# Group-norm sums between the steps of a convolution stack: operands in float32r pieces, and the mean's sum one step later

## The chip, the cores and the metric

The kernel runs on one core of one Trainium2 chip. The metric is the time of one execution on the device, in microseconds; a result is the median of several runs. Engines have names in the profile: PE is TensorE (PEld its weight loads), DVE is VectorE, ACT is ScalarE, POOL is GpSimd, SP is SyncE, which issues most transfers.

## The reference: what is computed

The input `x` has four batches of 32 x 32 points with 16 channels. Three layers of the same kind come first, each `x = x + conv(gn(x))`. `gn` is a group norm: for each batch and each pair of channels, mean and variance are taken over all 1024 points and both channels.

```
g = v.reshape(B_, H_, W_, G, C_ // G)
m = jnp.mean(g, axis=(1, 2, 4), keepdims=True)
s = jnp.var(g, axis=(1, 2, 4), keepdims=True)
return ((g - m) / jnp.sqrt(s + eps)).reshape(v.shape)
```

The convolution has its own 3 x 3 filter `G` for each of the 1024 points that it looks from; what each filter makes of the whole image is subtracted from the input, cut off at zero, weighted with `Wp` and summed; a term with `M` is added. The fourth layer is a long two-dimensional filter whose taps come from a quotient of Fourier transforms. It too begins with a group norm.

## The kernel before, in words

**Layout.** The 128 partitions of an activation tile are eight rows of points times sixteen channels; the free axis has four batches of 128 points each. The batches are worked on in two pairs: pair 0 is batches 0 and 1, pair 1 is batches 2 and 3.

**A layer.** `conv_layer` (L433) goes through 128 blocks, eight to a chunk of weights. What is called a step here is one block for one batch: six matmuls (L470): two row halves of 64 partitions for each of three weight tiles. `ga` and `gb` are float32, `gn` is float32r. Each float32 matmul leaves two records in the profile, each float32r matmul one, so a step has ten records. They accumulate in a pair of PSUM banks. VectorE then reduces the pair against the weights `wt` (L478, output `junk`, the sum in `acc`). The PSUM pool holds four such pairs (`pair_psum`, L70), for the group norm's sums too.

**The order is written by hand.** Nothing is planned: instructions stand on each engine in the order in which the Python code issues them. After each step, `step()` (L426) moves every generator in the list `todo` to its next `yield`. That is how side work gets between the steps.

**The ends of a pair.** The jobs of a layer are sorted so that pair 0 ends eight blocks (sixteen steps) before pair 1 does: in the first two and the last two jobs, only one pair is worked on. When a pair is done, VectorE adds the result to the residual (L493), and `finish` is put on `todo` and moved once at once. In layers 0 and 1 `finish` is `make_image` (L268): a group norm, then `store_image` (L276), which writes the normalised pair to DRAM (L288 on SP, L289 and L290 on ACT), then `load_image` (L292), which loads it again in 24 shifted copies through SP, ACT and POOL (L301). The next layer's matmuls on that pair need these copies. In layer 2 `finish` is `norm3` (L730), which normalises into VectorE's own tiles for the last filter. Other side work of the page, such as `beside` (L440), isn't touched.

**The group norm.** `group_norm` (L108) has four parts, with `yield` between them: statistics of the pair (`bn_stats`, L116); sums of the means over partitions by TensorE, then the mean and the deviations `d` on VectorE (L121 to L128); sums of `d`; the variance and its inverse root (L133 to L144). `group_sums` (L98) makes the sums: one float32 matmul of the operand with the constant table `avg` for each row half, `lhsT=avg[rows], rhs=s[rows]` (L105). For a pair the operand has four columns. `norm3` uses another way for pair 1, `column_sums` (L733). The first norm of all, in `first_images` (L167), is over four batches at once, before the first step; `rest` (L239) inside it is side work of the first steps.

Between the mean's sums and the variance's, `make_image` has two steps (two `yield`s, L129 and L130). `norm3` has one for pair 0, since it takes the first of the two itself.

Of the kernel before, what the change touches and what calls it, by code (L numbers as in the profile page):

```python
# [29 lines left out]
F32 = mybir.dt.float32  # L30
F32R = mybir.dt.float32r
AF = mybir.ActivationFunctionType
ALU = mybir.AluOpType
AX = mybir.AxisListType
# [3 lines left out]
P = 128  # L38
B, C, S = 4, 16, 32
# [15 lines left out]
def conv_stack_kernel(ctx, tc, x, raw, M, W, G, den, num, h0, cst, dft, one, idp, idq, out):  # L55
    nc = tc.nc

    const = ctx.enter_context(tc.tile_pool(name="const", bufs=1))
    xp = ctx.enter_context(tc.tile_pool(name="xp", bufs=2))
    work = ctx.enter_context(tc.tile_pool(name="work", bufs=1))  # L60
    small = ctx.enter_context(tc.tile_pool(name="small", bufs=2))
# [8 lines left out]
    def pair_psum():  # L70
        return ps.tile([P, 2, 512], F32, tag="pt", name="pt")
# [5 lines left out]
    xs = xp.tile([P, B, NBLK], F32, tag="x", name="x")  # L77
    nc.sync.dma_start(out=xs, in_=x)
    cs = const.tile([P, 2 * P + C + 2], F32, name="cs")
    nc.scalar.dma_start(out=cs, in_=cst)  # L80
    ident, avg, mid = cs[:, :P], cs[:, P : 2 * P], cs[:, 2 * P : 2 * P + C]
    is_lo, sign = cs[:, 2 * P + C : 2 * P + C + 1], cs[:, 2 * P + C + 1 :]


# [20 lines left out]
            nc.tensor.matmul(pt[:, h, :n], lhsT=avg[rows], rhs=s[rows], start=True, stop=True)  # L105
        return pt[:, :, :n].rearrange("p h (b e) -> p b h e", e=2), AX.XY

    def group_norm(xt, center=None, sums=group_sums):  # L108


        nb = xt.shape[1]
        vec = lambda name: small.tile([P, B], F32, tag=name, name=name)[:, :nb]

        st = small.tile([P, B, 2, 3], F32, tag="st", name="st")[:, :nb]
        for b in range(nb):
            nc.vector.bn_stats(st[:, b].rearrange("p e k -> p (e k)"), xt[:, b])  # L116
        half, m, m2 = NBLK // 2, st[:, :, :, 1], st[:, :, :, 2]
        yield
        pm, axes = sums(m)
        neg = vec("neg")  # L120
        nc.vector.tensor_reduce(neg, pm, axes, ALU.add)  # L121
        nc.vector.tensor_scalar(neg, neg, -float(half), None, ALU.mult)
        if center:
            center(neg)
        d = small.tile([P, B, 2], F32, tag="d", name="d")[:, :nb]
        nc.vector.tensor_tensor(d, m, neg.unsqueeze(2).to_broadcast([P, nb, 2]), ALU.add)
        nc.vector.tensor_tensor(d, d, d, ALU.mult)
        nc.vector.scalar_tensor_tensor(d, d, float(half), m2, ALU.mult, ALU.add)  # L128
        yield  # L129
        yield  # L130
        pv, axes = sums(d)
        v = vec("v")
        nc.vector.tensor_reduce(v, pv, axes, ALU.add)  # L133
        nc.vector.tensor_scalar(v, v, 1e-5, None, ALU.add)

        r = vec("r")
        nc.scalar.activation(r, v, AF.Sqrt)
        ri = vec("ri")
        nc.vector.reciprocal(ri, r)
        nc.vector.tensor_tensor(ri, ri, v, ALU.mult)  # L140
        nc.vector.tensor_tensor(r, r, ri, ALU.add)
        nc.vector.tensor_scalar(r, r, 0.5, None, ALU.mult)
        rstd = vec("rstd")
        nc.vector.reciprocal(rstd, r)  # L144
        return neg, rstd
# [21 lines left out]
    def first_images():  # L167

        of = lambda t, b: t[:, :, b % 2].rearrange("p l cc x -> p l (cc x)")
        rlo = st.tile([P, B], F32, name="rlo")  # L170

        def center(which, *batches):
            for b in batches:
                v = of(ims[b // 2][which], b)
                nc.scalar.activation(v, v, AF.Identity, bias=neg[:, b : b + 1])  # L175

        def scale(b):
            v = of(ims[b // 2][1], b)
            nc.scalar.activation(v, v, AF.Copy, scale=rstd[:, b : b + 1])  # L179

        def clear(which, a, b=slice(0, 2)):

            top, bottom = (0, 0, slice(0, S)), (3, 3, slice(0, S))
            left, right = ((slice(0, 4), slice(0, 4), slice(x, x + 1)) for x in (0, S - 1))
            parts = {
                0: [(g, g + 16, left) for g in range(0, P, 32)] + [(0, 32, top)],
                1: [(g, g + 32, right) for g in (0, 64)]
                + [(g + 32, g + 48, left) for g in (0, 64)]
                + [(0, 16, top), (96, P, bottom)],
                2: [(0, P, right), (64, P, bottom)],  # L190
            }[which]
            for lo, hi, (l, cc, x) in parts:
                nc.gpsimd.memset(ims[a][which].bitcast(F32)[lo:hi, l, b, cc, x], 0.0)  # L193

        def first_tap(b):
            v = of(ims[b // 2][0], b)
            nc.vector.tensor_scalar(v, v, rstd[:, b : b + 1], None, ALU.mult)

        def last_tap(b):

            v, v8, m = of(nine[b // 2], b), of(ims[b // 2][2], b), neg[:, b : b + 1]
            nc.vector.tensor_scalar(v8, v, m, rstd[:, b : b + 1], ALU.add, ALU.mult)
            yield
            nc.vector.tensor_scalar(v, v, m, rlo[:, b : b + 1], ALU.add, ALU.mult)
            yield
            nc.vector.scalar_tensor_tensor(v8, v8.bitcast(F32), sign, v, ALU.mult, ALU.add)
            clear(2, b // 2, slice(b % 2, b % 2 + 1))

        first, second = (prepare_g(0, 0, part) for part in halves)
        neg = None  # L210

        def early(mean):
            nonlocal neg
            neg = mean
            center(0, 0, 1)
            clear(0, 0)
            next(first)

        norm = group_norm(xs, early)
        while True:  # L220
            try:
                next(norm)
            except StopIteration as end:
                neg, rstd = end.value
                break
        for b in range(2):
            center(1, b)
            clear(1, 0, slice(b, b + 1))
        scale(0)
        first_tap(0)  # L230
        nc.vector.tensor_scalar(rlo, rstd, is_lo, None, ALU.mult)
        list(last_tap(0))
        list(first)
        scale(1)
        first_tap(1)
        list(last_tap(1))
        next(second)

        def rest():  # L239

            yield
            list(second)
            yield
            for which in range(2):
                center(which, 2, 3)
                clear(which, 1)
            yield
            for _ in range(4):
                yield
            for b in (2, 3):  # L250
                scale(b)
                first_tap(b)
                yield
                yield from last_tap(b)
                yield
            for a in range(2):
                normalise(a, xs[:, 2 * a : 2 * a + 2], *(t[:, 2 * a : 2 * a + 2] for t in (neg, rstd)))
                yield

        todo.append(rest())  # L260

    def normalise(a, xt, neg, rstd):
        yc[a] = work.tile([P, 2, NBLK], F32, tag=f"yc{a}", name=f"yc{a}")
        for b in range(2):
            at = slice(b, b + 1)
            nc.vector.tensor_scalar(yc[a][:, b], xt[:, b], neg[:, at], rstd[:, at], ALU.add, ALU.mult)

    def make_image(a, xt):  # L268

        xt = xt[:, 2 * a : 2 * a + 2]  # L270
        neg, rstd = yield from group_norm(xt)
        store_image(a, xt, neg, rstd)
        yield
        load_image(a)
# [114 lines left out]
    def prepare_g(layer, ch, part=slice(0, GC)):  # L389


        at = chunk(layer, ch)
        if at[0] == 3 or (part.start == 0 and at in gt):
            return
        if part.start == 0:
            gt[at] = *gr[at][:2], gs.tile([P, GC, P], F32R, tag="gn", name="gn")
        ga, gb, gn = (t[:, part] for t in gt[at])
        g9 = gr[at][2][:, part]

        gv = ga.rearrange("r n (p f) -> r (n p) f", f=C)  # L400
        nc.gpsimd.tensor_tensor(  # L401
            gv, gv, mid.unsqueeze(1).to_broadcast([P, gv.shape[1], C]), ALU.subtract
        )
        yield
        nc.scalar.copy(gn, g9)  # L405
        for r in (32, 96):
            lo = gn[r : r + 32]
            nc.vector.tensor_tensor(lo, g9[r : r + 32], lo.bitcast(F32), ALU.subtract)  # L408
# [237 lines left out]
    with tc.tile_pool(name="st", bufs=1) as st:  # L646
# [20 lines left out]
        xs = conv_layer(0, xs, make_image, impulse_response())  # L667
    xs = conv_layer(1, xs, make_image)
# [37 lines left out]
    early, then = ([of_pair(a, k, q) for k, q in ((1, 0), (1, 2), (0, 0))] for a in range(2))  # L706
# [23 lines left out]
    def norm3(a, xt):  # L730
# [15 lines left out]
        if a == 0:  # L746
# [1 line left out]
            yp = yp[:, : 16 * (31 + S - FIRST)]  # L748
            late["yp"] = yp.rearrange("p (a cc q b) -> p a cc q b", a=2, cc=4, b=2)
            nc.gpsimd.memset(late["yp"], 0.0)  # L750
        steps = group_norm(xt[:, 2 * a : 2 * a + 2], sums=column_sums if a else group_sums)
        if a:
            xr = work.tile([P, 4, S, B], F32, tag="ft", name="xr")
            nc.scalar.copy(xr, xt.rearrange("p b (cc q) -> p cc q b", q=S))
            late["sides"] = pair_psum()
            bank_of.update({("pair", n): late["sides"][:, n] for n in range(2)})
            run(early[0])
        next(steps)
        yield
        next(steps)  # L760
        if a:
            run(early[1])
# [54 lines left out]
    xs = conv_layer(2, xs, norm3, toeplitz(), late_toeplitz())  # L817
# [5 lines left out]
    pt = pair_psum()  # L823
# [130 lines left out]
```

## Time and profile before

| what | value |
|---|---|
| median of 3 runs | 3122.62 us (3121.87 to 3123.34) |
| the profiled execution's own time | 3123.33 us |
| its span, first to last instruction | 3121.6 us |
| granted TensorE clock | 1.000 |
| group-norm sums at L105, matmul records | 48 (24 on `st`, 24 on `d`) |
| TensorE idle before L105 for the statistics L116 | 7.7 us in 6 places, of them 5.4 us at the start |
| mean of one L478 reduction on VectorE | 1224 ns |

A line of a group of instructions has the source line, the engine, the operation, output and inputs with their shapes, and the count; then the busy time in us and the mean duration in ns; then the engine's idle time just before, and what ended most of it. A line of the chain of waits has the start in us, the duration in us and what ran. A line of the timeline has start, duration, engine, line and operation; a bracket gives the idle time before it and what ended it.

### The profile page before, as it was taken

What the parts mean: (1) busy time and instruction counts of PE and PEld (TensorE: products, weight loads), DVE (VectorE), ACT (ScalarE), POOL (GpSimd) and SP (SyncE); (2) the same over time, 40 slices, a digit from 0 to 9 for tenths busy, and PEclk for the clock granted to TensorE, in tenths of its full rate; (3) what the DMA queues carried; (4) which work ended last, traced back from release to release, by engine and by line L of the source; (5) the groups of instructions that cost most, each with busy time, mean ns of one, the idle gap of its engine ahead of it and who ended that gap; (6) DMA issues with size and microseconds to landing.
All of it is one profiled execution on the core that took longest, in us unless ns stands there. A gap on an engine that the chain in (4) does not pass through costs nothing.

```text
span 3121.6 us, 39186 instructions
## 1 busy us (share of the span) xinstructions
PE 3105.2 (99%) x16264; PEld 1668.7 (53%) x16264; DVE 2066.5 (66%) x3341; ACT 82.4 (3%) x107; POOL 236.8 (8%) x271
## 2 busy tenths in 40 slices
PE   8999999999999999999999999999999999999999
PEld 4445567777777554444444444455444444444444
DVE  7666766666667666666666666766666666666664
ACT  1000000000000000000000000000000000000000
POOL 1012321000000100100000000010010000000000
PEclk9999999999999999999999999999999999999999
DMA  8453355333332654433333333275543444444422
GB/s 216 133 124 87 81 118 123 90 88 88 100 92 66 144 133 131 95 88 88 101 92 88 87 101 91 69 144 128 140 105 97 96 109 107 96 97 106 109 44 42
DMA packets 68406, 322.77 MB, mean 103 GB/s; under 512 B 10514, under 2 KB 17556, under 8 KB 42756
## 3 DMA queue, kind: packets, MB, share of 16 engines
q1 hardware_dynamic: 57280, 301.61, 38.9%
q10 hardware_dynamic: 6612, 10.94, 2.0%
q0 software_dynamic: 4336, 7.72, 1.4%
q8 instruction: 127, 2.08, 0.3%
q14 instruction: 51, 0.42, 0.1%
HBM read 313.82 MB, written 6.41 MB: 103 GB/s over the span
## 4 chain that ended last, share of the span: by engine, by line
PE 99%; DVE 0%; DMA 0%; POOL 0%; issue 0%; ACT 0%; SPq 0%; POOLq 0%; DVEq 0%; ACTq 0%
PE pt L470 96%; PE pt L721 1%; PE pt L335 1%; DVE junk L478 0%; DMA im<-in_raw_dram 0%; PE pt L523 0%; PE pt L566 0%; PE pt L605 0%; PE pt L105 0%; POOL im L193 0%; DVE x L493 0%; DVE st L116 0%; PE pt L323 0%; ACT im L175 0%; ACT im L179 0%
## 5 line engine op out<-in xcount | busy, mean ns | idle before, releaser
L478 DVE SCALAR_TENSOR_TENSOR junk<-pt,w 128x1024 f32<-128x1024 f32 x1536 | 1880.7, 1224 | 993.5 <-PE pt L470 979.5
L470 PE MATMUL pt<-im,ga 64*128 64x512 f32 x6144 | 1676.0, 591 | 3.1 <-POOL im L193 3.1
L470 PE MATMUL pt<-im,gb 64*128 64x512 f32 x6144 | 1668.1, 588 | 0.1
L470 PE MATMUL pt<-im,gn 64*128 64x512 f32 x3072 | 1342.6, 806 | 0.0
L470 PEld LDWEIGHTS pt<-im,gb 64*128 64x128 f32 x6144 | 674.9, 185 | 669.5 <-issue 586.9
L470 PEld LDWEIGHTS pt<-im,ga 64*128 64x128 f32 x6144 | 671.6, 187 | 389.7 <-DVE junk L478 219.5
L470 PEld LDWEIGHTS pt<-im,gn 64*128 64x128 f32 x3072 | 350.6, 186 | 332.7 <-issue 291.5
L401 POOL TENSOR_TENSOR ga<-ga,cs 128x1024 f32<-128x1024 f32 (+2 forms) x49 | 113.5, 2317 | 2088.6 <-DMA ga<-in_G_dram 2088.3
L478 DVE DVE_READ_ACCUMULATOR junk<-pt,w 128x1 f32 x1536 | 127.8, 83 | 0.0
L408 DVE TENSOR_TENSOR gn<-g,gn 32x1024 fp32r<-32x1024 f32 (+2 forms) x98 | 118.4, 1208 | 4.7 <-ACT gn L405 2.5
L405 ACT CAST gn<-g 128x1024 fp32r<-128x1024 f32 (+2 forms) x49 | 50.4, 1029 | 2257.9 <-DMA g<-in_G_dram 1755.4
L359 POOL DMA_DIRECT2D fd<-ft x48 | 25.2, 533 | 223.3 <-DVE ft L352 222.1
L721 PE MATMUL pt<-t,y 128*32 128x512 f32 (+3 forms) x352 | 23.9, 432 | 0.0
L335 PE MATMUL pt<-mt,yt 128*64 128x512 f32 x96 | 21.9, 598 | 0.0
L721 PEld LDWEIGHTS pt<-t,y 128*32 128x32 f32 x352 | 11.0, 110 | 12.7 <-issue 10.8
L842 DVE TENSOR_TENSOR xo<-xo,both 128x512 f32<-128x512 f32 x2 | 1.4, 692 | 23.5 <-DMA both<-sd 23.5
L301 POOL DMA_DIRECT2D im<-img x32 | 16.1, 513 | 8.9 <-DMA img<-y 8.9
L721 PE MATMUL pt<-t,yp 128*32 128x512 f32 (+3 forms) x192 | 13.6, 434 | 0.2 <-DVE yp L771 0.2
L335 PEld LDWEIGHTS pt<-mt,yt 128*64 128x64 f32 x96 | 6.4, 136 | 13.7 <-issue 9.7
L544 POOL TENSOR_TENSOR H<-H,d 128x256 f32<-128x256 f32 (+1 forms) x10 | 8.2, 824 | 68.2 <-DVE d L549 67.8
L284 POOL COPY e<-y 32x612 f32<-32x612 f32 x4 | 2.8, 693 | 126.5 <-DVE y L283 126.5
L544 POOL TENSOR_TENSOR t<-s 128x256 f32<-128x256 f32 (+1 forms) x15 | 11.3, 753 | 0.0
(92 smaller groups left out, 209.2 us busy)
## 6 DMA issues: line engine op xcount, KB each, us to landing
w<-in_W_dram SPq DMA_DIRECT2D x192, 1024.0 KB, 7.5
ga<-in_G_dram SPq DMA_DIRECT2D x47, 512.0 KB, 3.5
gb<-in_G_dram SPq DMA_DIRECT2D x47, 512.0 KB, 4.3
g<-in_G_dram SPq DMA_DIRECT2D x47, 512.0 KB, 7.2
mt<-in_M_dram SPq DMA_DIRECT2D x24, 512.0 KB, 10.0
t<-hd ACTq DMA_DIRECT2D x28, 160.0 KB, 7.4
t<-hd SPq DMA_DIRECT2D x28, 160.0 KB, 8.4
im<-img SPq DMA_DIRECT2D x32, 67.5 KB, 5.4
```

Source lines behind the costliest of these rows:

```text
L284: nc.gpsimd.tensor_copy(ye[a][96:, :, :, 1:, :], ys[a][96:, :, :, :3, :])
L301: (nc.sync, nc.scalar, nc.gpsimd)[n % 3].dma_start(out=ims[a][k][at : at + C] .bitcast(F32) .rearrange("c l b cc x -> c l (b cc x)")[:, :, ...
L335: nc.tensor.matmul(pf[64 * h : 64 * h + 64], lhsT=yt[:, 4 * part + k].rearrange("k b c -> k (b c)"), rhs=mts[k][:, h, :], start=(k == 0), ...
L359: nc.gpsimd.dma_start(out=fv[h, cc, b], in_=ft[at : at + C, cc])
L401: nc.gpsimd.tensor_tensor(gv, gv, mid.unsqueeze(1).to_broadcast([P, gv.shape[1], C]), ALU.subtract)
L405: nc.scalar.copy(gn, g9)
L408: nc.vector.tensor_tensor(lo, g9[r : r + 32], lo.bitcast(F32), ALU.subtract)
L470: nc.tensor.matmul(pt[:, half, :], lhsT=w[rows, blk % GC, :], rhs=im[rows, :, b % 2, :, :S], start=n == 0, stop=n == 2,)
L478: nc.vector.scalar_tensor_tensor(junk, pt.rearrange("p h m -> p (h m)"), 0.0, wt, ALU.min, ALU.mult, accum_out=acc[b // 2][:, b % 2, blk : ...
L544: mul = lambda o, u, w: nc.gpsimd.tensor_tensor(o, u, w, ALU.mult)
L721: nc.tensor.matmul(rows.rearrange("n (j r) -> n j r", j=C)[:, :, 8 * cc :], lhsT=y(cc).rearrange("p q b -> p (q b)"), rhs=ts[k][q][:, :, : ...
L842: nc.vector.tensor_tensor(xo, xo, both[:, bass.ts(i, S * C)], ALU.add)
```

## The change

Two new functions stand beside `group_sums`. `in_pieces` splits a float32 operand into two float32r pieces on VectorE: `hi` is the operand rounded to float32r, and `lo` is what is left of it. The four columns of a pair become eight. `piece_sums` multiplies these eight columns with `avg_r`, a float32r copy of the table `avg`; VectorE's reductions after it (L121 and L133) then add over four instead of two values for each batch. Both hi and lo go through one float32r matmul for each row half.

`group_norm` gets the preparation of the operand as an argument of its own, `operand`, and calls it right after the operand is there. It has one more `yield` between the statistics and the mean's sums. Pieces are what it does unless told otherwise. The first norm of all keeps `group_sums` on the unsplit operand, and so does `column_sums` for pair 1 of `norm3`. The table's copy is made on VectorE at the end of `rest`.

`norm3` runs the first two parts with a step after each for pair 0; for pair 1 it runs them one right after the other, as the one part before.

```diff
+    avg_r = const.tile([P, P], F32R, name="avg_r")
...
-    def group_norm(xt, center=None, sums=group_sums):
+    def in_pieces(s):
+
+        pieces = small.tile([P, B, 2, 2], F32R, tag="pieces", name="pieces")[:, : s.shape[1]]
+        hi, lo = pieces[:, :, 0], pieces[:, :, 1]
+        nc.vector.tensor_copy(hi, s)
+        nc.vector.tensor_tensor(lo, s, hi.bitcast(F32), ALU.subtract)
+        return pieces
+
+    def piece_sums(pieces):
+
+
+        pt = pair_psum()
+        n = 4 * pieces.shape[1]
+        for h in range(2):
+            rows = slice(64 * h, 64 * h + 64)
+            nc.tensor.matmul(
+                pt[:, h, :n],
+                lhsT=avg_r[rows],
+                rhs=pieces[rows].rearrange("p b k e -> p (b k e)"),
+                start=True,
+                stop=True,
+            )
+        return pt[:, :, :n].rearrange("p h (b e) -> p b h e", e=4), AX.XY
+
+    def as_it_is(s):
+        return s
+
+    def group_norm(xt, center=None, operand=in_pieces, sums=piece_sums):
...
         half, m, m2 = NBLK // 2, st[:, :, :, 1], st[:, :, :, 2]
+        to_add = operand(m)
         yield
-        pm, axes = sums(m)
+        yield
+        pm, axes = sums(to_add)
...
         nc.vector.scalar_tensor_tensor(d, d, float(half), m2, ALU.mult, ALU.add)
+        to_add = operand(d)
         yield
         yield
-        pv, axes = sums(d)
+        pv, axes = sums(to_add)
...
-        norm = group_norm(xs, early)
+        norm = group_norm(xs, early, as_it_is, group_sums)
...
+            nc.vector.tensor_copy(avg_r, avg)
...
-        steps = group_norm(xt[:, 2 * a : 2 * a + 2], sums=column_sums if a else group_sums)
+        ways = dict(operand=as_it_is, sums=column_sums) if a else {}
+        steps = group_norm(xt[:, 2 * a : 2 * a + 2], **ways)
...
-        next(steps)
-        yield
+        for _ in range(2):
+            next(steps)
+            if not a:
+                yield
         next(steps)
```

## The prediction

> **What bounds the kernel.** I read the page first: busy times, the shares of the chain that ended last, the costliest groups.
>
> ```profile
> PE 3105.2 (99%) x16264; PEld 1668.7 (53%) x16264; DVE 2066.5 (66%) x3341; ACT 82.4 (3%) x107; POOL 236.8 (8%) x271
> ...
> PE 99%; DVE 0%; DMA 0%; POOL 0%; issue 0%; ACT 0%; SPq 0%; POOLq 0%; DVEq 0%; ACTq 0%
> ...
> L478 DVE SCALAR_TENSOR_TENSOR junk<-pt,w 128x1024 f32<-128x1024 f32 x1536 | 1880.7, 1224 | 993.5 <-PE pt L470 979.5
> ```
>
> TensorE is 99% of the chain; VectorE mostly waits for it. So only what TensorE executes, or waits for, counts. Next, the chain around one end of a batch pair (layer 0 into 1), where the sums of the change stand:
>
> ```profile
> 1009.10 1.24 DVE junk L478 x2
> ...
> 1010.36 0.44 DVE x L493
> ...
> 1010.83 0.50 DVE st L116 x2
> 1011.32 0.14 issue
> 1011.46 0.39 PE pt L105 x4
> 1011.85 4.00 PE pt L470 x18
> 1015.85 0.15 PE pt L105 x2
> ```
>
> Here the chain leaves TensorE: it goes through the last reduction of the pair, the residual addition L493 and the statistics L116 before the mean sums (L105) may start. The variance sums at 1015.85 have no VectorE piece ahead of them. The timeline gives the size. Of each step I take the last matmul on `gn`:
>
> ```profile
> 1010.21 0.80 PE L470 MATMUL pt<-im,gn 64*128 64x512 f32 x1
> ...
> 1011.46 0.39 PE L105 MATMUL pt<-st,cs 64*128 64x4 f32 x4 [0.45 <-DVE st L116]
> ...
> 1013.11 0.81 PE L470 MATMUL pt<-im,gn 64*128 64x512 f32 x1
> ...
> 1015.07 0.81 PE L470 MATMUL pt<-im,gn 64*128 64x512 f32 x1
> ...
> 1017.27 0.80 PE L470 MATMUL pt<-im,gn 64*128 64x512 f32 x1
> ```
>
> An undisturbed step is 1.963 us (elsewhere the chain has 120 matmul records, twelve steps, in 23.56 us; here 1013.11 to 1015.07). The step with the mean sums takes 2.90, the one with the variance sums 2.20. So mean sums cost about 0.93 us, most of it a stall, and variance sums 0.23 us with no stall. Third, VectorE at the end of layer 2:
>
> ```profile
> 3042.69 0.49 DVE L116 BATCH_NORM_STATS2 st<-x 128x6 f32<-128x128 f32 x2
> 3043.09 1.21 DVE L478 SCALAR_TENSOR_TENSOR junk<-pt,w 128x1024 f32<-128x1024 f32 x1
> ...
> 3044.23 0.16 DVE L121 TENSOR_REDUCE neg<-pt 128x2 f32<-128x8 f32 x1
> ...
> 3045.02 0.17 DVE L128 SCALAR_TENSOR_TENSOR d<-d,st 128x4 f32<-128x4 f32 x1
> 3045.82 1.23 DVE L478 SCALAR_TENSOR_TENSOR junk<-pt,w 128x1024 f32<-128x1024 f32 x1 [0.63 <-PE pt L470]
> ```
>
> The reader is to see the spacing: five small operations from 3044.23 to 3045.02, one each 0.2 us, and the next reduction that TensorE releases at 3045.82.
>
> [...] each `ga` or `gb` matmul leaves two records (6144 for 3072), each `gn` (float32r) one; `ga` to `gb` is 0.86 us. [...] The variance sums have four loads on two row halves[...]. [...]
>
> **The change, part by part.** Five group norms are touched: both pairs at the ends of layers 0 and 1, and the first pair of layer 2. The very first norm and the last pair keep their sums.
>
> 1. Removed: five stalled mean sums. From one reduction that TensorE released to the one two steps on: 1009.10 to 1013.95, 1041.66 to 1046.52, 2024.96 to 2029.88, 2057.60 to 2062.45, 3040.89 to 3045.82. Less 2 x 1.963 = 3.926 that is 0.92, 0.93, 0.99, 0.92 and 1.00. Five variance sums at 0.23 go too.
> 2. Added on TensorE: ten pairs of float32r matmuls of eight columns, one record and one load for each half instead of two. The trace has no such matmul. Bounds: 0 (loads wholly hidden) and 0.23 (something other than the loads sets the price). I take half of 0.23, 0.115, since records and loads halve[...].
> 3. Added on VectorE: two small operations before each sum, 0.4 us, 20 in all, and one 128x128 copy of the table (the 128x256 cast at L281 is 0.29). Hidden: VectorE idles 0.73 us in a normal step. At the copy (about 53 us) it is late by the rest of a queue, but an idle 0.32 follows. Bare, they would be 20 x 0.2 + 0.3 = 4.3 us. Behind them in VectorE's order wait the reductions (L478), and TensorE waits for those only through the four PSUM pairs. Worked through below, the tightest of these has over 2 us left.
> 4. Moved: mean sums one step later. When are the pieces ready? In the first four norms statistics end at 1011.32 (first case); two operations make it about 1011.7; the sums are wanted at the end of the next step, 1012.97 less the 0.20 us by which unstalled sums start ahead of it (1015.68 against the modelled end 1015.88). 1.1 us to spare, no stall. The variance follows two steps later as before. VectorE: pieces to 3043.58 (times of layer 2, which differ little), two reductions at 3043.5 and 3044.87 (1.33 apart), mean from 3046.01, five small operations and two for the pieces, ready 3047.35. Wanted 3048.6: no stall.
> 5. The fifth norm has only one step between mean and variance sums, before and after. Now the mean comes after two reductions, not one, and two pieces follow it. Last matmul end before the variance sums: 3042.82 + 2 x 1.963 + 0.115 = 3046.86. Ready is 3047.35. How stalls are priced: in the first case data were ready 0.31 us after the matmul's end (1011.01), sums started 0.14 later, that is 0.65 later than unstalled ones, and cost 0.69 more. So a stall costs readiness less end, plus 0.34, plus 0.04. Here 0.49 + 0.38 = 0.87, plus 0.115: 0.99. The stall moves from mean to variance and stays about as long.
>
> What the delay pushes back: variance read about 1.1 us later against the first stalled point, while the next layer comes about 0.9 + 0.1 us sooner, 2.1 us of the image path's slack. Stores (L288, L289) and the 24 image loads (L301) on SP, ACT and POOL move; behind them on SP stand W and G loads. First pair: transfers end by about 1034.2 (DMA share 0.07 to there, 0.00 after), used at 1041.42: 7.2 becomes 5.1. Second pair: last issue 1061.6, landing up to 7 us, wanted 1073.99: about 5.4 becomes 3.3. The W loads behind them are for blocks some 60 us on. PSUM: the variance sums' buffer comes back to use four allocations on; mean read by 3.4 us after the first step's end, next use 6.0.
>
> Sum: first four norms, 3.76 + 4 x 0.23 = 4.68 removed, 8 x 0.115 = 0.92 added: 3.76 saved. Fifth: 1.00 + 0.23 removed, 0.115 + 0.99 added: 0.13 saved. Together 3.9 us, 0.12%. The profiled execution took 3123.33 with a span of 3121.6 (1.7 around it); it should become 3119.4 with a span of 3117.7. It lies 0.7 above the median of 3122.62; the median should be **3118.7**.
>
> **Rivals.**
> - No stall in the fifth norm: if the pieces there are ready by 3046.5, another 0.87 is saved: 3117.9. For it: VectorE starts a reduction up to 0.09 us before its forerunner ends. Against: 0.83 us of VectorE work would have to vanish. 12%.
> - Float32r sums as dear as before (0.23): 10 x 0.115 less saved, 3119.9. For it: the weight loads of `gn` are recorded at 186 ns like all others. 15%. If instead they are nearly free, 3117.6; 4%.
> - The stalls stay: another wait than the statistics holds the mean sums. Against: TensorE's idle time there names L116 and starts 0.14 us after it. 3122.6; 4%.
> - Slower: images come too late. Its place is the first matmul on a pair's new image, at four boundaries: two with 5.1 us of slack left, two with 3.3. If loads land L us later than worked out, the loss is about 2 x (L - 3.3) + 2 x (L - 5.1). That eats the 3.9 at L = 5.2 and makes 0.2% slower than before at L = 6.7 (10.1 us lost, 3128.8). For it: the DMA share is 0.98 to 1.26 while images load, so lateness can feed on itself. Against: the trains shift by only 2 us, and nothing joins them. 3%.
>
> The likeliest keeps 62%.
>
> **How the numbers follow.** What can be told from no change is about 0.2%, 6.2 us. The largest gain from every term at its best is 3.9 + 0.87 + 1.15 = 5.9, so faster by over 0.2% needs a scatter on top (runs spread 1.5): 3%. Slower is the last rival: 3%. The rest, 94%, is within. The range holds the first two rivals and the likeliest, with a scatter of 0.9: 3117.0 to 3120.8.
>
> **What would show it.** In the new profile: steps with sums of about 2.08 us in the first four norms; no VectorE piece of the chain ahead of their mean sums; half as many records for sums; in the last norm before the end, a variance sum that waits for the pieces, its step about 2.95 us. Wrong: a stall at the mean sums, a variance sum of layer 2 without wait, a wait for an image at a layer's first matmul, or ten sums at 0.23.

## The result, and the profile after

The changed kernel takes 3118.48 us, the median of 20 runs (3118.01 to 3120.05); the kernel before took 3122.65 us in as many runs. The ratio is 0.9987 with a 95% interval of 0.9981 to 0.9993. The forecast was 3118.7 us and a saving of 3.9 us; 4.2 was measured between the medians. It is a small gain, below the 0.2% that was named as the bound for telling it from no change, but the interval leaves 1 out.

Lines have moved in the source: the matmuls of a step are at L503 now, the reductions at L511, the statistics at L144, the pieces at L113 and L114, and the new sums at L124. First the page of the kernel after, two of the lines shown of before:

```profile
PE 3102.1 (100%) x16244; PEld 1698.8 (55%) x16244; DVE 2069.1 (66%) x3362; ACT 82.4 (3%) x107; POOL 236.7 (8%) x271
...
PE 99%; DVE 0%; DMA 0%; POOL 0%; issue 0%; ACT 0%; SPq 0%; POOLq 0%; ACTq 0%
```

TensorE has 20 records fewer (half of the 40 that the ten sums left before), VectorE 21 more. TensorE is still the chain. Then the chain of waits in the stretch that answers to the one shown of before, the end of pair 0 in layer 0:

```profile
1004.96 14.15 PE pt L503 x69
```

It is one piece. The last reduction, the residual addition and the statistics, which stood in the chain before, are gone from it. The timeline of the same stretch has the sizes, again by the last matmul on `gn` of each step:

```profile
1008.76 0.81 PE L503 MATMUL pt<-im,gn 64*128 64x512 f32 x1
...
1010.10 0.16 DVE L114 TENSOR_TENSOR pieces<-st,pieces 128x4 fp32r<-128x4 f32 x1
...
1010.72 0.81 PE L503 MATMUL pt<-im,gn 64*128 64x512 f32 x1
...
1011.00 0.17 PE L124 MATMUL pt<-pieces,avg_r 64*128 64x8 f32 x1
...
1012.80 0.81 PE L503 MATMUL pt<-im,gn 64*128 64x512 f32 x1
...
1014.76 0.81 PE L503 MATMUL pt<-im,gn 64*128 64x512 f32 x1
...
1016.84 0.81 PE L503 MATMUL pt<-im,gn 64*128 64x512 f32 x1
```

The pieces are done at 1010.26, the mean's sums start at 1011.00 with no wait, and both steps with sums take 2.08 us (1010.72 to 1012.80, 1014.76 to 1016.84) instead of 2.90 and 2.20. The other six sums of the first four norms take 2.07 to 2.08 too. The fifth group norm, pair 0 of layer 2, looks different:

```profile
3038.78 0.82 PE L503 MATMUL pt<-im,gn 64*128 64x512 f32 x2
...
3040.86 0.82 PE L503 MATMUL pt<-im,gn 64*128 64x512 f32 x2
...
3042.00 0.16 DVE L114 TENSOR_TENSOR pieces<-d,pieces 128x4 fp32r<-128x4 f32 x1
...
3042.31 0.27 PE L124 MATMUL pt<-pieces,avg_r 64*128 64x8 f32 x2 [0.62 <-DVE pieces L114]
...
3043.84 0.81 PE L503 MATMUL pt<-im,gn 64*128 64x512 f32 x1
```

Here the mean's step is 2.08 us, but the variance's step takes 2.98: TensorE idles 0.62 us for the pieces of `d`. Before, they were 2.97 and 2.19. The stall has moved, not gone.

**Where the time went.** The span went from 3121.6 to 3116.3, 5.3 us. Not all of that is the change. The chains of the two kernels give the start of layer 0's first transposes, which stand ahead of any touched group norm, and the first matmul of the last filter (before, then after):

```profile
92.99 0.59 PE pt L323 x4
...
3073.49 2.29 PE pt L721 x32
```

```profile
91.48 0.59 PE pt L356 x4
...
3068.21 2.29 PE pt L754 x32
```

From one to the other it is 2980.50 us before and 2976.73 after: 3.77 us saved. This stretch is called the loop below. It repeats well: a second profile of the changed kernel (last experiment) has 2976.68. The other 1.5 us lie ahead of the loop, where the change has nothing but the table's copy, and they scatter: in that second profile the transposes start at 92.16. In the first, the image load in the chain landed 0.66 us sooner than in the profile of before (6.53 against 7.19), and the first pair of `gn` matmuls is recorded at 0.82 us where that of before has 1.42. This scatter can account for the 4.2 and 5.3 that medians and spans say.

### The profile page after: what moved, and what is told of

Its sections match the earlier page's. It is cut to its first block, busy times and chain, and to the rows that moved or that the text cites. A ratio compares the mean times of both kernels' runs of the same rounds, so it can differ in the third digit from the quotient of the medians.

```text
span 3116.3 us, 39167 instructions
## 1 busy us (share of the span) xinstructions
PE 3102.1 (100%) x16244; PEld 1698.8 (55%) x16244; DVE 2069.1 (66%) x3362; ACT 82.4 (3%) x107; POOL 236.7 (8%) x271
## 3 DMA queue, kind: packets, MB, share of 16 engines
q8 instruction: 127, 2.08, 0.3%
## 4 chain that ended last, share of the span: by engine, by line
PE 99%; DVE 0%; DMA 0%; POOL 0%; issue 0%; ACT 0%; SPq 0%; POOLq 0%; ACTq 0%
PE pt L503 97%; PE pt L754 1%; PE pt L368 1%; DMA im<-in_raw_dram 0%; PE pt L556 0%; PE pt L599 0%; PE pt L638 0%; POOL im L224 0%; PE pt L356 0%; ACT im L206 0%; DVE junk L511 0%; DVE gn L441 0%; DVE im L237 0%; POOL ga L434 0%; DVE xo L889 0%
## 5 line engine op out<-in xcount | busy, mean ns | idle before, releaser
L511 DVE SCALAR_TENSOR_TENSOR junk<-pt,w 128x1024 f32<-128x1024 f32 x1536 | 1880.1, 1224 | 983.9 <-PE pt L503 967.0
L503 PE MATMUL pt<-im,ga 64*128 64x512 f32 x6144 | 1711.0, 590 | 2.8 <-POOL im L224 2.8
L503 PE MATMUL pt<-im,gb 64*128 64x512 f32 x6144 | 1703.3, 588 | 0.1
L503 PE MATMUL pt<-im,gn 64*128 64x512 f32 x3072 | 1377.7, 805 | 0.2 <-POOL im L224 0.2
L503 PEld LDWEIGHTS pt<-im,gb 64*128 64x128 f32 x6144 | 696.0, 185 | 662.0 <-issue 637.6
L503 PEld LDWEIGHTS pt<-im,ga 64*128 64x128 f32 x6144 | 707.8, 187 | 368.2 <-DVE junk L511 214.0
L503 PEld LDWEIGHTS pt<-im,gn 64*128 64x128 f32 x3072 | 368.7, 186 | 330.0 <-issue 317.0
L511 DVE DVE_READ_ACCUMULATOR junk<-pt,w 128x1 f32 x1536 | 126.9, 83 | 0.0
L754 PEld LDWEIGHTS pt<-t,y 128*32 128x32 f32 x352 | 10.9, 110 | 12.8 <-issue 10.9
```

Of the source, the lines that this page charges most:

```text
L503: nc.tensor.matmul(pt[:, half, :], lhsT=w[rows, blk % GC, :], rhs=im[rows, :, b % 2, :, :S], start=n == 0, stop=n == 2,)
L511: nc.vector.scalar_tensor_tensor(junk, pt.rearrange("p h m -> p (h m)"), 0.0, wt, ALU.min, ALU.mult, accum_out=acc[b // 2][:, b % 2, blk : ...
L754: nc.tensor.matmul(rows.rearrange("n (j r) -> n j r", j=C)[:, :, 8 * cc :], lhsT=y(cc).rearrange("p q b -> p (q b)"), rhs=ts[k][q][:, :, : ...
```

## The experiments

Every version was measured on the same chip as the kernel before, which had medians of 3122.2 to 3122.4 us there. Loop lengths come from one profile of each version. The differences of the medians from the kernel before agree with those of the loops within about 0.5 us, but for the sums five times over and the later images.

**The extra step alone.** The five norms keep float32 sums on the unsplit operand.

```diff
-    def group_norm(xt, center=None, operand=in_pieces, sums=piece_sums):
+    def group_norm(xt, center=None, operand=as_it_is, sums=group_sums):
```

> The extra step alone: the five group norms keep their float32 sums on the unsplit operand, and the mean's sums come one step later. My account: in the first four norms the mean's stall goes (0.94 to 0.23 us each, 2.8 saved). In the fifth the mean costs 0.23 and the variance sums wait about 0.3 us for VectorE (step of about 2.5 us), 0.45 saved. Together 3.3 saved against before, about 3119.4 us, so 0.6 to 0.9 slower than the changed kernel. Rival, that float32r with half as many loads is what pays: within 0.5 us of before (3122 to 3123). Rival, that only the later place counts: as the changed kernel, 3118.5.

Measured: 3119.34 us, ratio 0.9991 (0.9984 to 0.9997); the loop is 2977.23, 3.27 us shorter than before. In the timeline of this version's fifth norm, steps by their last `gn` matmul:

```profile
3039.95 0.81 PE L503 MATMUL pt<-im,gn 64*128 64x512 f32 x2
...
3042.13 0.81 PE L503 MATMUL pt<-im,gn 64*128 64x512 f32 x2
...
3043.05 0.39 PE L106 MATMUL pt<-d,cs 64*128 64x4 f32 x4
...
3044.70 0.80 PE L503 MATMUL pt<-im,gn 64*128 64x512 f32 x1
```

2.18 us for the mean's step and 2.57 for the variance's; 2.5 was expected for the latter. So the later place is worth 3.3 of the 3.8 us. The pieces add half a us net: they make the sums cheaper by about 0.1 each (steps of 2.18 become 2.08) and lengthen the fifth norm's wait.

**The pieces alone.** The mean's sums stay one step after the statistics.

```diff
         to_add = operand(m)
         yield
-        yield
         pm, axes = sums(to_add)
...
-        for _ in range(2):
-            next(steps)
-            if not a:
-                yield
+        next(steps)
+        yield
         next(steps)
```

> The float32r pieces alone, with the mean's sums one step after the statistics as before the change. My account: two more VectorE operations (0.4 us) stand between the statistics and the sums on the path, the stall grows by them, and each sum is 0.115 cheaper. First four norms: +0.17 each. Fifth: mean +0.29, and a new wait of about 0.3 us ahead of the variance sums, +0.5. Together about 1.2 us slower than before: 3123.8. Steps with the mean's sums about 3.19 us, with the variance sums 2.08. Rival, that the pieces by themselves save: 3121.5 or less.

Measured: 3123.91 us, ratio 1.0005 (0.9997 to 1.0013); the loop is 2981.73, 1.23 us longer than before. The ratio alone is unclear; the loop and the chain are not. The chain of this version at the end of pair 0 of layer 2:

```profile
3042.59 0.50 DVE st L144 x2
...
3043.11 0.18 DVE pieces L113
...
3043.32 0.17 DVE pieces L114
3043.49 0.14 issue
3043.63 0.27 PE pt L124 x2
```

The two operations that make the pieces stand in the chain, 0.4 us between statistics and sums. The steps with the mean's sums take 3.18 to 3.24 us, as expected (3.19). The cheaper sums don't pay for that. Uncovered, the pieces cost more than they save here.

**Two steps in the fifth norm.** The changed kernel, and pair 0 of layer 2 has the same distance between its sums as the other norms.

```diff
+        if not a:
+            yield
         neg, rstd = yield from steps
```

> The changed kernel, but pair 0 of layer 2 gets two steps between the mean's and the variance's sums, as the other four norms have. My account: the wait of the variance sums for the pieces (0.62 us of idle TensorE, a step of 2.98 us) goes, that step becomes 2.08, and nothing else is late: 0.9 us faster than the changed kernel, about 3117.6. Rival, that another wait takes its place (the pair's normalised tiles come a step later for the last filter): as the changed kernel, 3118.5.

Measured: 3117.86 us, ratio 0.9986 (0.998 to 0.9993); the loop is 2975.84, 0.89 us shorter than the changed kernel's. Its timeline at the fifth norm:

```profile
3040.97 0.82 PE L503 MATMUL pt<-im,gn 64*128 64x512 f32 x2
...
3042.93 0.82 PE L503 MATMUL pt<-im,gn 64*128 64x512 f32 x2
3043.58 0.18 PE L124 MATMUL pt<-pieces,avg_r 64*128 64x8 f32 x2
...
3045.01 0.82 PE L503 MATMUL pt<-im,gn 64*128 64x512 f32 x2
```

An undisturbed step of 1.96, then one of 2.08 with the sums, and no wait. So 0.89 us was the price of the stall that had moved, and nothing takes it back. Without pieces a second step there would save about 0.4 us (2.57 less 2.18), an estimate that no run tests. So where nothing waits, the pieces are worth about 1.0 us of the 4.66 that this version saves against before.

**The sums five times over.** Each sum's matmuls are issued five times; the last one counts.

```diff
-        for h in range(2):
+        for h in 5 * [0, 1]:
```

> The changed kernel with each sum's two float32r matmuls issued five times over (same operands and place, the result is that of the last): eight more loads and matmuls in each of ten sums. [...] If the 0.115 us is a fixed price of breaking the stream of steps, not of loads, further pairs cost little: 3118.5 to 3119.5, steps below 2.2 us.

Measured: 3123.84 us, ratio 1.0005 (0.9997 to 1.0013); the loop is 2980.71, 3.98 us longer than the changed kernel's. The timeline at pair 0 of layer 0:

```profile
1010.81 0.81 PE L503 MATMUL pt<-im,gn 64*128 64x512 f32 x1
1011.13 0.83 PE L124 MATMUL pt<-pieces,avg_r 64*128 64x8 f32 x9
...
1013.33 0.81 PE L503 MATMUL pt<-im,gn 64*128 64x512 f32 x1
```

The step is 2.52 us, 0.44 more than with one pair: 0.11 us for each further pair of loads and matmuls. That is near the 0.115 us that the prediction took (four further pairs at 0.115 would be 0.46), and it grows with their count, so it isn't a fixed price of breaking the stream. Loads and matmuls were multiplied together; which of the two sets it is not shown. Nine sums at 0.44 make 3.96 us. The tenth, the fifth norm's variance, cost nothing here: longer sums of the mean let VectorE catch up, and the wait for the pieces fell from 0.62 to 0.18 us. The medians say more than the loop: this one lies 5.0 us above the higher of the changed kernel's two (3118.48 and 3118.84). The profiled execution, with 3122.17 us, was the fastest of its 13 runs, and what the others lose beyond is in no profile.

**One matmul of 128 rows.** The two halves of a sum become one.

```diff
-        for h in range(2):
-            rows = slice(64 * h, 64 * h + 64)
-            nc.tensor.matmul(
-                pt[:, h, :n],
-                lhsT=avg_r[rows],
...
+        nc.tensor.matmul(
+            pt[:, 0, :n],
+            lhsT=avg_r,
...
```

> The changed kernel with one float32r matmul of 128 rows for each sum instead of one for each half of 64 rows. If [...] the two halves' loads run side by side, one load of 128 rows costs what two of 64 do: steps with sums of about 2.08 us in layer 2, where the halves run in phase, up to 0.3 us more in layer 0, where they are some 0.3 us apart in the trace and have to be brought together. If the halves' loads run one after the other at half the price each, or the price goes by the count of instructions, one is cheaper: about 2.02 us.

Measured in a single run: 3120.25 us; its loop is 2979.02, 2.29 us longer than the changed kernel's. The timeline in layer 2:

```profile
3040.92 0.82 PE L501 MATMUL pt<-im,gn 64*128 64x512 f32 x2
...
3041.67 0.19 PEld L122 LDWEIGHTS pt<-pieces,avg_r 128*128 128x128 f32 x1 [0.57 <-issue]
...
3043.29 0.81 PE L501 MATMUL pt<-im,gn 64*128 64x512 f32 x2
```

A step with sums takes 2.37 us, also in layer 2, where both halves run in phase. Both expectations missed. The weight load starts 0.57 us after the one before it ended, against 0.23 for the loads of halves there, and the sums cost 0.41 us in place of 0.115. The load itself is recorded at 0.19 us, no longer than one of 64 rows. In layer 0 the last `gn` matmuls of the two halves start 0.32 us apart ahead of the sum (1010.26 and 1010.58) and together behind it (1012.94). What holds the load back is not shown.

**Images later.** Two versions test the rival that ends slower. `make_image` waits two or four steps more before it stores.

```diff
         neg, rstd = yield from group_norm(xt)
+        for _ in range(2):
+            yield
```

> The changed kernel with the image's store and loads of layers 0 and 1 two steps (3.9 us) later. My account of the image path: after the change the loads have landed about 5 to 6 us before the next layer needs them, so nothing waits: 3118.5, as the changed kernel. The prediction's figure for the second pair (3.3 us left) would give about 1.3 us more: 3119.8. Rival, that the image path already is at its limit: 4 x 3.9 = 15.7 us more.

> The same with four steps (7.85 us) later. Beyond the slack, each us costs 1 us at each of four boundaries. With 5.1 and 3.3 us of slack (the prediction's figures) 2 x 2.75 + 2 x 4.55 = 14.6 us more, 3133; with 5 to 6.5 us, as the changed kernel's own trace suggests, 5 to 11 us more, 3124 to 3129. The trace should show waits for images at the first matmuls on a pair. If nothing is lost, the slack was over 7.9 us: 3118.5.

Neither version delays the images by as much as was expected. From the mean's sums to the store it is 8.5 to 8.9 us in the changed kernel, 10.9 to 11.2 with two steps and 14.8 to 15.1 with four: about 2.4 and 6.3 us later, not 3.9 and 7.85.

Two steps: 3120.86 us, ratio 0.9996 (0.9987 to 1.0004), some 2 us above the changed kernel. The profiled execution was the fastest of its runs and lost only 0.34 us in the loop; that the others waited for images is likely but no profile shows it. What it lost stands at the second pairs, in steps of 2.08 and 2.26 us instead of 1.96; at the first pairs it lost nothing. But the edit also changes the order on SP. SP's part of the timeline, the changed kernel for both pairs and this one for the second:

```profile
1019.86 0.33 SPq L321 DMA_DIRECT2D img<-y  x1
1022.34 7.70 SPq L334 DMA_DIRECT2D im<-img  x8
1030.54 1.19 SPq L451 DMA_DIRECT2D w<-in_W_dram  x2
1051.49 0.35 SPq L321 DMA_DIRECT2D img<-y  x1
1053.95 6.01 SPq L334 DMA_DIRECT2D im<-img  x8
1061.31 0.35 SPq L419 DMA_DIRECT2D ga<-in_G_dram  x1
```

```profile
1054.63 0.35 SPq L323 DMA_DIRECT2D img<-y  x1
1055.08 0.37 SPq L421 DMA_DIRECT2D ga<-in_G_dram  x1
...
1057.36 13.01 SPq L336 DMA_DIRECT2D im<-img  x8
```

Three G loads now stand ahead of the second pair's image loads, and these take 13.01 us to issue instead of 6.01. So this version doesn't measure how much slack the changed kernel has.

Four steps: 3147.57 us, ratio 1.008 (1.0066 to 1.0094), with a loop 28.1 us longer, twice the 14.6 that the prediction's formula gives for 7.85 us. Two things had been left out of it. First the order on SP again, here for the first pair:

```profile
1026.50 0.33 SPq L323 DMA_DIRECT2D img<-y  x1
1026.88 0.55 SPq L453 DMA_DIRECT2D w<-in_W_dram  x1
1029.16 12.37 SPq L336 DMA_DIRECT2D im<-img  x8
```

At all four boundaries a W load of 1 MB stands ahead of the image loads, and at this one these take 12.37 us to issue instead of 7.70. TensorE waits for images at each of the four, 4.99 us at the first. Second, the matmuls behind the wait ran at a lower granted clock. The timeline of the first boundary, then the table of stretches (after its bounds: length, then busy us of PE, PEld, DVE, ACT and POOL, then the granted clock, the DMA share and GB/s):

```profile
1044.55 2.17 PE L505 MATMUL pt<-im,ga 64*128 64x512 f32 x4 [4.99 <-DMA im<-img]
```

```profile
1036.00:1039.00 3.00, 3.00 (x19) 2.40 (x15) 2.14 (x4) 0.00 (x0) 0.60 (x2) 1.00 1.07 142
...
1044.50:1046.50 2.00, 1.95 (x5) 1.20 (x7) 0.00 (x0) 0.00 (x0) 0.00 (x0) 0.50 1.01 229
...
1048.50:1050.50 2.00, 2.00 (x12) 1.25 (x9) 1.23 (x2) 0.00 (x0) 0.00 (x0) 0.71 0.84 240
```

After 4.99 us of idle the granted clock is 0.50, and it comes back at about 1049.7, an estimate from the mean of 0.71 in the last stretch. From the end of the wait to the last `gn` matmul of the second step behind it are 5.91 us (1044.55 to 1050.46); at the undisturbed pace of before (1.36 us from a step's first matmul to its last, then 1.96) it would be 3.32. So the wait and the lower clock cost 4.99 and 2.6 us at this boundary, 7.6 together. The 28.1 us over four boundaries are 7.0 each; how the other three divide is in none of the views here.

**Twice the pieces' work on VectorE.** Both operations that make the pieces are issued twice.

```diff
-        nc.vector.tensor_copy(hi, s)
-        nc.vector.tensor_tensor(lo, s, hi.bitcast(F32), ALU.subtract)
+        for _ in range(2):
+            nc.vector.tensor_copy(hi, s)
+            nc.vector.tensor_tensor(lo, s, hi.bitcast(F32), ALU.subtract)
```

> The changed kernel with the two VectorE operations that make the pieces issued twice over: 0.4 us more of VectorE ahead of each of ten sums. If VectorE's work is hidden as worked out, the first four norms lose nothing (1.1 us to spare at the mean, 1.2 at the variance, of which 0.4 and 0.8 are used), and the fifth loses 0.8 at the variance sums: about 3119.3. If added VectorE work is on the path: ten times 0.4, 3122.5.

Measured: 3119.65 us, ratio 0.9991 (0.9983 to 0.9999); the loop is 2977.51, 0.78 us longer than the changed kernel's. The timeline shows where:

```profile
3043.51 0.27 PE L125 MATMUL pt<-pieces,avg_r 64*128 64x8 f32 x2 [1.42 <-DVE pieces L115]
```

The wait in the fifth norm grew from 0.62 to 1.42 us, and that is all: 4 us more of VectorE's work cost 0.8, in the one place that had no cover.

**Side by side.** The changed kernel and the version with two steps in the fifth norm, on one chip.

> The changed kernel itself, beside the version with two steps in the last touched norm, on one chip: about 4 us below the kernel before.

> The version with two steps between mean and variance sums for pair 0 of layer 2 again, now beside the changed kernel. If the trace's step of 2.08 us instead of 2.98 is worth its time, it is 0.9 us faster than the changed kernel on the same chip, 4.6 to 4.9 below the kernel before. If the rest of the kernel takes the time back, the two agree within 0.3 us.

Measured: 3118.84 us (ratio 0.9989, 0.9982 to 0.9995) and 3117.94 us (0.9986, 0.9979 to 0.9993), 0.90 apart; loops of 2976.68 and 2975.83. The version with two steps is the fastest of all.

## Why the prediction was right

The measured median is 0.2 us from the forecast. That it is so close is in part luck, since the changed kernel's two medians alone are 0.36 us apart. But the parts of the sum hold one by one.

- **Removed: five stalled mean sums.** The extra step alone gave 3.27 us in the loop, where 3.3 was expected from the same working. That the stall was one of VectorE's chain (reduction, addition, statistics) is shown from the other side by the pieces alone: lengthening the chain by 0.4 us made the loop 1.23 us longer.
- **Added on TensorE: 0.115 us a sum.** The choice lay between 0 and 0.23. Steps with sums take 2.08 us, and repeating the sums gives 0.11 for each further pair. The rival "as dear as before" and the one "nearly free" both fall. The half was the author's estimate, from records and loads that halve (four of each for a float32 sum on `d`, two for one on pieces); whether loads or matmuls set the price is not shown.
- **Added on VectorE: hidden.** In the first four norms the pieces are ready 0.7 to 1.3 us ahead of the sums (1.1 had been worked out for the mean's). Twice the work cost these norms nothing.
- **The table's copy: right about its cost, wrong about its cover.** It took 0.21 us at 51.66, while VectorE was still late, and the idle 0.32 us expected behind it was not there in that execution: three reductions follow back to back. TensorE was busy all the same through the 16 us from 44 to 60, so the copy is hidden, but not by that gap. That PSUM's four pairs carried the delay is argued, not shown by a run.
- **The fifth norm: the stall moves.** Expected was a variance step of 2.95 us; it is 2.98. The rival without a stall falls, and giving this norm a second step brings 0.89 us, where 0.87 had been worked out.
- **The slower rival: right to be unlikely, wrong in its price.** The image path was not late: TensorE never waits for an image in the changed kernel's loop. The slacks of 5.1 and 3.3 us stay untested, since both later versions put weight loads ahead of image loads, which the change itself does not. What failed is the price of 1 us for each us late: at the first boundary of the version with four steps an idle of 4.99 us cost 7.6, with the matmuls after it at a granted clock of 0.50.
- **The sum.** 3.9 us were worked out; the loops of the two profiles give 3.77 and 3.82. The rest of the 4.2 us between the medians lies within the scatter of the time ahead of the loop (91.48 and 92.16 in the changed kernel's two profiles).

## What to carry to other kernels

On an engine that is busy all the time, look for the few places where its chain leaves it, and ask for each how long another engine works from the last input to the operand. If that is longer than the work still queued, put one more piece of work ahead of it; then follow the next operand in the same way, since a stall that is moved ahead of a shorter distance can come back there, as the 0.62 us of idle in the fifth norm did. Preparing an operand to make a short matmul cheaper paid here only where the preparation itself was covered: about 1.0 us saved over ten sums where nothing waits (the estimate above), 1.23 us lost in the loop where the pieces stand between statistics and sums.

## What the runs showed of the hardware

- A sum over 128 rows in one matmul cost 0.41 us between steps made of two 64-row halves, against 0.115 us for two matmuls of 64 rows. The load of 128 rows is recorded at 0.19 us, like one of 64.
- After 4.99 us without a matmul the granted TensorE clock was 0.50 for the next 4 us, and the mean was 0.71 in the 2 us after them. With a wait for images at each of four boundaries the loop took 28.1 us more.
- The loop of some 2977 us repeats closely: 0.05 us lie between two profiles of the changed kernel, 0.01 between two of the version with two steps. What comes ahead of it, while the first inputs land, spread by 1.6 us over the profiles (91.38 to 92.99).
